# Reordering four pieces of a fused attention and feed-forward block: the turns of y, a maximum's transpose, the pairs' statistics and the adding of y's rows

## The chip, the cores and the metric

The kernel runs on one core of one Trainium2 chip. The metric is the device time in microseconds of the whole program; lower is better. Three runs of the kernel before gave 776.5, 776.8 and 777.04 us, so the median is 776.8 us.

## The reference

The block takes x with 8 batch entries of 1024 rows and 256 columns, all in float32. Cut to what matters:

```python
h = layernorm(x) * (1 + ca) + sa
lhs, rhs = h * w_lhs, h * w_rhs
attn = softmax(einsum('nsd,ntd->nst', lhs, rhs), axis=2)
x = x + ga * einsum('nst,ntd->nsd', attn, h)
h = layernorm(x) * (1 + cb) + sb
y = relu(h @ W1 + b1) @ W2 + b2          # W1: 256 x 1024, W2: 1024 x 256
x = x + gb * y
```

The six rows sa, ca, ga, sb, cb, gb of each batch entry come from a small product of silu(c) and wmod; ga and gb are kept at least 0.25 away from zero.

## The kernel before, in words

**Tiling and order of the work.** A batch entry b (0 to 7) is worked in eight steps i (0 to 7), one for each block of 128 rows. Attention is done for entry b in its own steps; the feed-forward part of entry b-1 is woven into the same steps, its first half of 512 rows in steps 0 to 3 and its second half in steps 4 to 7. So entry b's steps hold attention of b, the feed-forward part of b-1, and the preparation of b+1. Entry 0 has a branch of its own, and the feed-forward part of entry 7 is a tail behind the loop. The order is written out by hand: a program-wide pin at the end ties every instruction to the one before it on its engine, so each engine executes in the order in which the source emits.

**A step in attention.** `direct` (L405, L412) makes the scores of a block that is two steps ahead, from the diagonal to the right. `mirror` (L428) turns that row block on the vector engine into a tile called Tm, and `move` (L295) writes it to DRAM (tile D_m) and reads it back into the column below the diagonal. `row_max` (L455) takes the maximum m of a row, `max_turn` (L460) turns it on TensorE into the PSUM tile pm, `subtract` (L467) and `exponent` (L476) make pT, and `product` (L488) and `product_out` (L502, L504, and the statistics L237, L238) make the new rows of x. In steps 2, 3, 6 and 7 two row blocks are worked together by a seven-product scheme: `pair_begin`, `left_sums`, `pair_end` (the products into pq and pr, L579), `pair_out` (eight vector instructions, L594 to L607) and `pair_stats` (the statistics of the pair, two times L237 and L238).

**A step in the feed-forward part.** In steps 0, 1, 4 and 5 (called "first" in the source) two pairs c of hidden blocks are made: `pair_products` (L713, tiles pa, pb, pc; `kept` is ScalarE's copy of pa), `pair_sums` (four vector instructions, L747, L750, L753, L756), `pair_last` (one product, L764 on the vector engine and L765 on GpSimd), `pair_relu` (L774, L775 on ScalarE) and `pair_turn` (four GpSimd additions, L784 to L787). `pair_products` takes a function `between`, which is the transpose of a maximum when it is given, and calls it right after pa's products. Steps 2, 3, 6 and 7 make y, transposed, in the tile Y (L803 to L838), and `y_turn` (L848) turns it on the vector engine into a tile T_y and moves it through DRAM (D_y) back into Y; `y_add` (L861) adds the rows on GpSimd and `y_out` (L864) stores x.

**Queues and buffers around the change.** All the writes and reads of `move` are issued by SyncE's queue (SP), in program order; a read waits on that queue until its writes have landed. A move with hurry=True issues its read at once, one with hurry=False puts it off until the next move has issued its own read. The tiles that the vector engine turns into (Tm, T_y, T_a, T_f) share one tag with two buffers:

```python
T = two.tile([P, NV, NT * V], F32, tag="T", name=f"T_y{b}_{g}")
```

and the PSUM tiles pa, pb, pc, po, pp, pq, pr and ya to yd share four buffers of the tag "a". In step 3 the tag T is used by Tm and then by T_y; in step 4 by Tm and then by T_a, the turn of the next entry's normalized rows (`prepare_blocks`, L317), which exists only where there is a next entry. In step 4 the vector engine's emitted order is: the sums of pair 0, Tm, L764, T_a, `subtract`, the sums of pair 1, L764, the statistics of the pair made in step 3, the maximum m, `product_out`. Step 5 follows with the second maximum and the sums of pair 2.

Of the kernel before, what the change touches and what calls it, by code (L numbers as in the profile page):

```python
# [24 lines left out]
def adaln_block_kernel(  # L25
# [14 lines left out]
    B, S, D = x.shape  # L40
    INTER = W1.shape[1]
    NT = S // P
# [3 lines left out]
    TH = HALF // P  # L46
    H2 = HALF // 2
    NH = NI // 2
    V = 32
# [245 lines left out]
    def move(out, blocks, m, name, hurry=True):  # L295


        D_ = dram.tile([NV, V, NV, NT * V], F32, tag="D", name=f"D_{name}", bufs=3)
        D_ = D_[:, :, :, 0:m]
        for a in range(NV):  # L300
            nc.sync.dma_start(
                out=D_[:, :, a, :].rearrange("b u m -> u b m"), in_=blocks[ts(a, V)]
            )
        read = lambda: nc.sync.dma_start(out=out, in_=D_.rearrange("b u a m -> (b u) a m"))
        if hurry:
            read()
            read_back()
        else:
            reads.append(read)
# [206 lines left out]
    def right_sums(b, which):  # L516

        xg = xg_t[b]
        b11, b12 = xg[:, 0:TH, P:D], xg[:, 0:TH, 0:P]
        b21, b22 = xg[:, TH:NT, P:D], xg[:, TH:NT, 0:P]  # L520
        t = [tsum[:, n, :, 0:P] for n in range(4)]
        ins = [(b12, b11), (b22, t[0]), (b22, b12), (t[1], b21)]
        for n in which:
            nc.gpsimd.tensor_tensor(t[n], *ins[n], ALU.subtract)

    halves = lambda pT: (pT[:, 0:TH, :], pT[:, TH:NT, :])
    two_t = {}
# [181 lines left out]
    lo, hi = slice(0, H2), slice(H2, HALF)  # L709
    pairs = {}  # L710

    def mm(out, lhsT, rhs):
        nc.tensor.matmul(out, lhsT=lhsT, rhs=rhs, start=True, stop=True)  # L713

    def pair_products(b, g, c, between=None):

        if c == 0:
            ffn["f"] = two.tile([P, NI, HALF], F32, tag="f", name=f"f_{b}_{g}", bufs=1)
            if b < B - 1:
                ffn["ft"] = two.tile([P, 3, NH, H2], F32, tag="ft", name=f"ft_{b}_{g}", bufs=1)  # L720
        hT, hs = ffn["hT", g]
        n = ts(c, P)
        s1, a22 = (w1[:, k, ds((c + NH) * P, P)] for k in range(2))

        pool, tag = (ps_s, "s") if b == B - 1 else (ps_a, "a")
        pa = ps_a.tile([P, HALF], F32, tag="a", name=f"pa_{b}_{g}_{c}")
        pb = pool.tile([P, HALF], F32, tag=tag, name=f"pb_{b}_{g}_{c}")
        pc = ps_a.tile([P, HALF], F32, tag="a", name=f"pc_{b}_{g}_{c}")
        mm(pa[:, lo], w1[:, 0, n], hT[:, 0, lo])
        mm(pa[:, hi], s1, hs[:, 0])  # L730
        kept = work.tile([P, HALF], F32, tag="kept", name=f"kept_{b}_{g}_{c}", bufs=3)
        nc.scalar.copy(kept, pa)  # L732
        if between:
            between()
        mm(pb[:, lo], w1s[:, 0, n], hs[:, 1])
        mm(pb[:, hi], w1s[:, 1, n], hs[:, 2])
        mm(pc[:, lo], w1[:, 1, n], hT[:, 1, lo])
        mm(pc[:, hi], a22, hT[:, 0, hi])
        pairs[c] = pa, pb, pc, kept
# [100 lines left out]
                scale=gcol[:, 0, h, b : b + 1], bias=gcol[:, 1, h, b : b + 1],  # L840
            )

    def y_turn(b, g):

        Y = ffn["Y"]
        T = two.tile([P, NV, NT * V], F32, tag="T", name=f"T_y{b}_{g}")
        for h in range(2):
            nc.vector.transpose(  # L848
                T.rearrange("p a (t h u) -> p a t h u", h=2, u=V)[:, :, :, h, :],
                Y[:, h].rearrange("p (t a v) -> p a t v", a=NV, v=V),  # L850
            )
        Y = Y.rearrange("p h r -> p (h r)").rearrange("p (b m) -> p b m", b=NV)
        move(Y, T, NT * V, f"y{b}_{g}", hurry=False)
        ffn["rows", b, g] = Y.rearrange("p b (t h u) -> p t h b u", h=2, u=V)

    def y_add(b, g, q):
# [278 lines left out]
    for b in range(B):  # L1135
        for i in range(NT):
# [4 lines left out]
            fb, fg = b - 1, i // TH  # L1141
# [54 lines left out]
            if first:  # L1196

                ub, ug = (b - 1, 0) if i >= TH else (b - 2, 1)
                back = i % TH == 0 and ub >= 0
                pair_products(fb, fg, c, turn_max)  # L1200
                if i == 0:
                    ffn_rstd(b - 1, 1)
                elif (b, i) == (B - 1, TH):
                    ffn_rstd(b, 0)
                if (b, i) == (1, 0):
                    weights(*late)
                    late = None
                if c > 0:
                    pair_relu(c - 1)
                pair_sums(fb, fg, c)  # L1210
                if ahead:
                    mirror(*ahead)
                pair_last(fb, fg, c)
                if i == 0:
                    right_sums(b, (3,))
                if c > 0:
                    pair_turn(c - 1)
                if i == 4 and b + 1 < B:
                    prepare_blocks(b + 1, 1)
                    xg_times(b + 1, 1)  # L1220
                if late:
                    subtract(*late)
                pair_products(fb, fg, c + 1, (lambda: max_turn(*extra)) if extra else None)
                pair_relu(c)
                sides_too = i == 4 and b + 1 < B
                if sides_too:
                    prepare_turn_apart(b + 1, 0, 1)
                if late:
                    exponent(*late)
                if sides_too:  # L1230
                    prepare_turn_apart(b + 1, 0, 0)
                middle(b, i)
                pair_sums(fb, fg, c + 1)
                pair_last(fb, fg, c + 1)
                if c == 0 and (b, i - 2) in two_t:
                    pair_stats(b, i - 2)
                if ahead and ahead != extra:
                    row_max(*ahead)
                pair_turn(c)
                if back:  # L1240
                    for q in range(2):
                        y_add(ub, ug, q)
                if i == 5:

                    turns(b, i)
                if c > 0:
                    pair_relu(c + 1)
                    pair_turn(c + 1)
            else:
                half = i % TH - 2  # L1250
                if i == 3 and b + 1 < B:
                    prepare_stats(b + 1, 1)
                if half == 0:
                    pair_begin(b, i, turn_max)
                elif not ahead:

                    pair_end(b, i - 1)
                    pair_out(b, i - 1)
                    pair_stats(b, i - 1)
                if half:  # L1260
                    y_second(fb, fg, turn_max)
                else:
                    y_first(fb, fg)
                if ahead:
                    mirror(*ahead)
                if i == 2 and b + 1 < B:
                    prepare_rstd(b + 1, 0)
                elif i == 3 and b + 1 < B:
                    prepare_rstd(b + 1, 1)
                elif i == 6 and b + 1 < B:  # L1270
                    ffn_rstd(b, 0)
                elif i == NT - 1 and b == B - 1:
                    ffn_rstd(b, 1)
                if half == 0:
                    pair_begin_sum(b, i)
                    if i == 2:
                        weights(*late)
                    left_sums(b, i)
                spare()
                early(b, i)  # L1280
                if late and i != 2:
                    weights(*late)
                middle(b, i)
                if i == 2 and b + 1 < B:
                    load_x(b + 1, 1)
                if i == 3 and b + 1 < B:
                    prepare_norm(b + 1, 1)
                    x_plus(b + 1, 1)
                spare()
                if ahead:  # L1290
                    row_max(*ahead)
                if half:
                    y_second_sums(fb)
                else:
                    y_first_sums()
                spare()
# [5 lines left out]
            if extra:  # L1302
                exponent(*extra)
            if not first:
                if half and b < B - 1 or i == 3:
                    y_turn(fb, fg)
                for _ in range(4 if half else 1):
                    spare()
            if first:
                product(b, i)  # L1310
                product_out(b, i)
            elif half and ahead:
                pair_end(b, i - 1)
                pair_out(b, i - 1)
                if i == NT - 1:
                    assert not queue
                    right_sums(b + 1, range(3))
                if i == NT - 1 or b == B - 1:
                    pair_stats(b, i - 1)
# [84 lines left out]
```

## Time and profile before

| what | value |
|---|---|
| median of three runs | 776.8 us (776.5 to 777.04) |
| profiled execution, its own time | 778.43 us |
| its span, first to last instruction | 776.6 us |
| clock granted to TensorE | 1.00 |
| TensorE products busy | 762.5 us |
| vector engine busy | 575.8 us |
| GpSimd busy | 534.0 us |
| ScalarE busy | 366.4 us |
| DMA | 95.18 MB, mean 123 GB/s |

The profiled execution is one run, 778.43 us in its own timing, of which 776.6 us lie between its first and its last instruction. The page lists busy time and, for groups of instructions, the idle time of the engine just before them and who ended it. The timeline view lists instructions of one engine in order of time, with start and length in us, and in square brackets an idle time before an instruction with its releaser. In this kernel one float32 product of 256 columns shows as two TensorE instructions.

### The profile page before, as it was taken

Reading aid. Unit: us, or ns where it says so; the run is one execution under the profiler, and the core shown is the slowest. Engines: PE = TensorE matmul, PEld = TensorE weight load, DVE = VectorE, ACT = ScalarE, POOL = GpSimd, SP = SyncE. Lnnn points to the kernel's source line nnn. Section 1 sums busy time; section 2 is a strip of 40 time slices with the busy share of each in tenths; the row PEclk is TensorE's granted clock in tenths of the full one; section 3 lists DMA queues with packets and bytes.
Section 4 is the critical chain, followed back from the end, with each engine's and each line's share of the span. In section 5 each row is a group of like instructions: output and inputs, shape, how many; then the busy total and the mean of one; then the engine's idle time right before and its main releaser. Section 6 shows DMA issues by size and latency. Waiting matters only on the chain.

```text
span 776.6 us, 11486 instructions
## 1 busy us (share of the span) xinstructions
PE 762.5 (98%) x3710; PEld 620.6 (80%) x3710; DVE 575.8 (74%) x1238; ACT 366.4 (47%) x671; POOL 534.0 (69%) x626
## 2 busy tenths in 40 slices
PE   8999999999999999999999999999999999999998
PEld 3576788788887888878887888878888788889886
DVE  6597879768796787957888677876879677594632
ACT  4464545535465355544546444553546535251511
POOL 0533895977949688586868778497694968559641
PEclk9999999999999999999999999999999999999999
DMA  5314434355344464434543544435444335232220
GB/s 190 124 28 149 123 103 119 122 167 169 95 128 126 130 177 113 144 104 125 169 126 116 150 149 129 110 121 177 139 121 125 107 122 170 58 103 86 81 82 27
DMA packets 106211, 95.18 MB, mean 123 GB/s; under 512 B 29700, under 2 KB 98848, under 8 KB 106152
## 3 DMA queue, kind: packets, MB, share of 16 engines
q1 hardware_dynamic: 98408, 85.81, 37.8%
q10 hardware_dynamic: 7744, 8.65, 3.5%
q8 instruction: 29, 0.48, 0.2%
q14 instruction: 30, 0.25, 0.1%
HBM read 50.62 MB, written 43.81 MB: 122 GB/s over the span
## 4 chain that ended last, share of the span: by engine, by line
PE 84%; DVE 10%; issue 2%; ACT 2%; POOL 1%; DMA 1%; SPq 0%; DVEq 0%; POOLq 0%
PE psc L405 14%; PE po L488 13%; PE pa L713 8%; PE pb L713 6%; PE yb L791 6%; PE ya L791 6%; PE pc L713 6%; PE yc L791 5%; PE pr L579 4%; PE pp L539 3%; PE py L896 3%; PE pq L579 3%; PE yd L791 3%; DVE pT L467 1%; DVE m L455 1%
## 5 line engine op out<-in xcount | busy, mean ns | idle before, releaser
L765 POOL TENSOR_TENSOR f<-f,kept 128x512 f32<-128x512 f32 x64 | 81.7, 1276 | 118.2 <-DVE f L764 89.6
L405 PE MATMUL psc<-rT,lT 128*128 128x512 f32 (+3 forms) x384 | 134.3, 486 | 0.0
L488 PE MATMUL po<-xg,pT 128*128 128x257 f32 x576 | 131.6, 380 | 0.0
L488 PEld LDWEIGHTS po<-xg,pT 128*128 128x128 f32 x576 | 108.8, 190 | 16.0 <-issue 1.0
L405 PEld LDWEIGHTS psc<-rT,lT 128*128 128x128 f32 x384 | 67.6, 190 | 38.1 <-issue 27.0
L412 ACT COPY sc<-psc 128x512 f32<-128x512 f32 (+3 forms) x96 | 44.8, 474 | 96.5 <-PE psc L405 96.5
L467 DVE TENSOR_TENSOR pT<-sc,pm 128x1024 f32<-128x1024 f32 x64 | 77.1, 1205 | 5.9 <-PE pm L460 5.8
L774 ACT ACTIVATE f<-f 128x512 f32<-128x512 f32 x64 | 40.4, 631 | 83.8 <-POOL f L765 83.8
L476 ACT ACTIVATE pT<-pT 128x1024 f32<-128x1024 f32 x64 | 67.0, 1047 | 26.4 <-DVE pT L467 26.4
L455 DVE TENSOR_REDUCE m<-sc 128x1 f32<-128x1024 f32 x64 | 77.1, 1205 | 0.0
L732 ACT COPY kept<-pa 128x512 f32<-128x512 f32 x64 | 37.4, 585 | 80.7 <-PE pa L713 80.7
L629 POOL TENSOR_TENSOR x<-x,rows 128x256 f32<-128x256 f32 x64 | 45.3, 740 | 37.4 <-ACT rows L1002 23.2
L713 PE MATMUL pb<-hs,w1s 128*128 128x256 f32 x256 | 67.1, 385 | 0.9 <-DVE f L750 0.6
L713 PE MATMUL pc<-hT,w 128*128 128x256 f32 x256 | 66.2, 381 | 0.0
L428 DVE STREAM_TRANSPOSE Tm<-sc 128x896 f32<-128x896 f32 (+6 forms) x49 | 34.7, 707 | 27.6 <-ACT sc L412 27.3
L713 PEld LDWEIGHTS pc<-hT,w 128*128 128x128 f32 x256 | 48.1, 190 | 7.7 <-ACT kept L732 1.4
L713 PEld LDWEIGHTS pb<-hs,w1s 128*128 128x128 f32 x256 | 45.5, 191 | 11.0 <-DVE f L750 4.6
L791 PE MATMUL yc<-f,w2s 128*128 128x256 f32 x224 | 52.1, 379 | 0.0
L791 PEld LDWEIGHTS yc<-f,w2s 128*128 128x128 f32 x224 | 41.5, 190 | 10.1 <-issue 2.9
L786 POOL TENSOR_TENSOR ft<-ft,f 128x256 f32<-128x256 f32 x56 | 41.9, 749 | 4.4
L785 POOL TENSOR_TENSOR ft<-ft,f 128x256 f32<-128x256 f32 x56 | 40.9, 730 | 4.4
L861 POOL TENSOR_TENSOR x<-x,Y 128x512 f32<-128x512 f32 x28 | 35.0, 1272 | 10.6 <-DMA Y<-D_y 10.6
(164 smaller groups left out, 1676.2 us busy)
## 6 DMA issues: line engine op xcount, KB each, us to landing
D_f<-T_f SPq DMA_DIRECT2D x60, 128.0 KB, 2.3
X_f<-D_f SPq DMA_DIRECT2D x15, 512.0 KB, 3.9
D_a<-T_a SPq DMA_DIRECT2D x56, 128.0 KB, 3.5
D_y<-T_y SPq DMA_DIRECT2D x56, 128.0 KB, 2.8
Y<-D_y SPq DMA_DIRECT2D x14, 512.0 KB, 3.9
out_dram<-x SPq DMA_DIRECT2D x14, 512.0 KB, 4.3
X_a<-D_a SPq DMA_DIRECT2D x13, 512.0 KB, 3.4
x<-in_L_attn_x_dram ACTq DMA_DIRECT2D x12, 512.0 KB, 3.8
```

Of the source, the lines that this page charges most:

```text
L405: nc.tensor.matmul(psc[:, : hi - lo], lhsT=lT_t[b, i // TH][:, k, ts(i % TH, P)], rhs=rT_t[b, n][:, k, lo - n * HALF : HALF], start=(k == ...
L412: nc.scalar.copy(score_row(b, i)[:, lo // V : hi // V, :], psc[:, : hi - lo].rearrange("p (n v) -> p n v", v=V),)
L455: nc.vector.tensor_reduce(m, score_row(b, i), AX.XY, ALU.max)
L467: nc.vector.tensor_tensor(pT.rearrange("p j (a v) -> p j a v", v=V), score_columns(b, i), pm[:, :P].rearrange("p (j a v) -> p j a v", j=1, ...
L476: nc.scalar.activation(pT_t[b, i], pT_t[b, i], AF.Exp)
L488: nc.tensor.matmul(po[:, : D + 1], lhsT=pT[:, t, :], rhs=xg_t[b][:, t, 0 : D + 1], start=(t == 0), stop=(t == NT - 1),)
L579: nc.tensor.matmul(out, lhsT=lhs[:, t, :], rhs=rhs[:, t, :], start=(t == 0), stop=(t == TH - 1),)
L629: queue.append(lambda: nc.gpsimd.tensor_tensor(out, in0, row, op))
L713: nc.tensor.matmul(out, lhsT=lhsT, rhs=rhs, start=True, stop=True)
L765: nc.gpsimd.tensor_tensor(f[:, c::NH, hi], f[:, c::NH, hi], kept[:, None, hi].to_broadcast([P, 2, H2]), ALU.add,)
L786: add(ft[:, 2, c], ft[:, 1, c], f[:, c + NH, lo], ALU.subtract)
L791: nc.tensor.matmul(out, lhsT=lhs(c), rhs=rhs(c), start=(c == 0), stop=(c == NH - 1))
```

## The change

The change touches only the order of emission. `pair_products` calls `between` after pb's two products and not before them. The statistics of the pair of step 3 (`pair_stats(b, 2)`) are emitted behind `product_out` of step 4 and no longer ahead of the maximum of step 4. In step 3 `y_turn` is emitted behind `pair_end` and `pair_out`, with its read put off as before; in step 7 it stays where it was, but its read is issued at once. In step 0 `y_add` moves from the end of the step to just behind `pair_last` of pair 0, `right_sums(b, (3,))` moves behind `pair_turn` of pair 0, and the relu and turn of pair 1 move from step 1 into step 0.

```diff
@@ pair_products
         nc.scalar.copy(kept, pa)
+        mm(pb[:, lo], w1s[:, 0, n], hs[:, 1])
+        mm(pb[:, hi], w1s[:, 1, n], hs[:, 2])
         if between:
             between()
-        mm(pb[:, lo], w1s[:, 0, n], hs[:, 1])
-        mm(pb[:, hi], w1s[:, 1, n], hs[:, 2])
@@ y_turn
-    def y_turn(b, g):
+    def y_turn(b, g, hurry=False):
...
-        move(Y, T, NT * V, f"y{b}_{g}", hurry=False)
+        move(Y, T, NT * V, f"y{b}_{g}", hurry)
@@ steps 0, 1, 4, 5
-                if c > 0:
+                if i == TH + 1:
                     pair_relu(c - 1)
                 pair_sums(fb, fg, c)
                 if ahead:
                     mirror(*ahead)
                 pair_last(fb, fg, c)
-                if i == 0:
-                    right_sums(b, (3,))
-                if c > 0:
+                if i == 0 and back:
+                    for q in range(2):
+                        y_add(ub, ug, q)
+                if i == TH + 1:
                     pair_turn(c - 1)
...
                 pair_last(fb, fg, c + 1)
-                if c == 0 and (b, i - 2) in two_t:
-                    pair_stats(b, i - 2)
                 if ahead and ahead != extra:
                     row_max(*ahead)
                 pair_turn(c)
-                if back:
+                if i == 0:
+                    right_sums(b, (3,))
+                    pair_relu(c + 1)
+                    pair_turn(c + 1)
+                elif back:
                     for q in range(2):
                         y_add(ub, ug, q)
@@ ends of the steps
             if not first:
-                if half and b < B - 1 or i == 3:
-                    y_turn(fb, fg)
+                if i == NT - 1 and b < B - 1:
+                    y_turn(fb, fg, True)
...
             if first:
                 product(b, i)
                 product_out(b, i)
+                if (b, i - 2) in two_t:
+                    pair_stats(b, i - 2)
             elif half and ahead:
                 pair_end(b, i - 1)
                 pair_out(b, i - 1)
+                if i < NT - 1:
+                    y_turn(fb, fg)
```

## The prediction

> **What bounds the kernel now.** I read the page's busy times first, then the list of waits for TensorE, then the timelines of TensorE, the vector engine and SyncE around steps 3 to 5.
>
> ```profile
> PE 762.5 (98%) x3710; PEld 620.6 (80%) x3710; DVE 575.8 (74%) x1238; ACT 366.4 (47%) x671; POOL 534.0 (69%) x626
> ```
>
> TensorE sets the time: what does not open or close one of its pauses moves nothing. From the list of waits (total us, times, longest):
>
> ```profile
> PE pm L460 <- DVE m L455: 3.9, 6, 1.1
> PEld pm L460 <- DVE m L455: 6.9, 7, 1.5
> PEld pb L713 <- DVE f L750: 4.6, 13, 0.8
> ```
>
> The pauses of entries 1 to 7 recur in two places. At entry 6, TensorE's timeline shows:
>
> ```profile
> 591.58 1.13 PE L713 MATMUL pb<-hs,w1s 128*128 128x256 f32 x4
> ...
> 598.18 0.59 PE L713 MATMUL pa<-hs,w 128*128 128x256 f32 x2
> 599.29 0.32 PE L460 MATMUL pm<-ident,m 128*128 128x128 f32 x1 [0.51 <-DVE m L455]
> ...
> 602.47 0.27 PE L460 MATMUL pm<-ident,m 128*128 128x128 f32 x1
> 602.59 1.13 PE L713 MATMUL pb<-hs,w1s 128*128 128x256 f32 x4
> ```
>
> A two-instruction group takes 0.43 us where nothing waits, so pm was due at 598.61: **0.67 us lost** at step 5. The pb at 591.58 (pair 1) came 0.21 us late, and the first half of a pb that waited costs 0.1 us more (1.13 against 1.03). The pb at 602.59 (pair 3) bears that mark too. The vector engine in the same stretch:
>
> ```profile
> 586.51 1.42 DVE L848 STREAM_TRANSPOSE T_y<-Y 128x512 f32<-128x512 f32 x2 [1.05 <-ACT Y L838]
> 587.85 0.26 DVE L594 TENSOR_TENSOR W<-pq,W 128x129 f32<-128x129 f32 x1
> ...
> 590.46 0.48 DVE L747 SCALAR_TENSOR_TENSOR u<-pb,cols,kept 128x256 f32<-128x256 f32 x1
> ...
> 592.70 1.29 DVE L317 STREAM_TRANSPOSE T_a<-xg 128x512 f32<-128x512 f32 x2
> ...
> 598.05 1.19 DVE L455 TENSOR_REDUCE m<-sc 128x1 f32<-128x1024 f32 x1
> ...
> 602.05 0.48 DVE L750 SCALAR_TENSOR_TENSOR f<-pb,b_step,u 128x256 f32<-128x256 f32 x1
> ```
>
> From T_y to L750 of pair 2, which ends at 602.53, the engine works without a pause. pb of pair 3 starts 0.06 us after that end. So it is **the vector engine's queue**, not the one maximum, that holds TensorE in steps 4 and 5. Entry 7 shows the same wait openly:
>
> ```profile
> 694.91 1.13 PE L713 MATMUL pb<-hs,w1s 128*128 128x256 f32 x4 [0.59 <-DVE f L750]
> ```
>
> A small natural experiment stands in entry 5, where T_a waited for its buffer:
>
> ```profile
> 500.32 1.30 DVE L317 STREAM_TRANSPOSE T_a<-xg 128x512 f32<-128x512 f32 x2 [0.51 <-DMA D_y<-T_y]
> ```
>
> There T_a came 7.78 us after the step's last product group (pr<-xg, 492.54) against 7.19 at entry 6 (585.51), 0.59 more; and TensorE's pause at pm was 1.28 against 0.67 us, 0.61 more. A late T_a is paid for one to one. In the trace, L750 of pair 2 ends 9.84 to 9.86 us after T_a's start in all of entries 1 to 6.
>
> **What the Trainium skill says.** "Perfetto Trace Analysis", section Optimization Strategy, says that a gap which repeats on the engine that should be saturated can mean too few buffers for the next tile. The trace agrees twice: pb waits for a PSUM buffer that L750 frees, T_a for one that D_y frees. "DMA: Bandwidth & Descriptors", section Anatomy of one DMA, puts about 2.0 us of fixed cost on a DMA, most of it the receipt of the last byte; it measured GpSimd's path. Here, from SyncE, the four 128 KB writes of D_y in step 3 show a median of 2.3 us to landing. "Trainium Architecture — The Big Picture", section Inside one NeuronCore, gives each engine its own instruction stream; the trace agrees in that everything behind the waiting T_a moved with it.
>
> **The change, part by part.**
>
> *The maximum's transpose two products later.* pm is due 4 × 0.216 = 0.86 us later (588.25 to 589.12 is one such pb group), enough for the 0.67 us. But pb of pair 3 then asks for its buffer earlier, and that buffer comes from L750 of pair 2, behind everything on the vector engine. Worth nothing by itself. pm of step 5's second maximum now also stands behind that pb, so its 0.11 us no longer lies in the pause: +0.11 us for each of entries 1 to 7.
>
> *Statistics later.* Two pairs of L237 and L238, 1.08 us (596.97 to 598.05), leave the place ahead of m of step 4, and land ahead of the second m (600.42). Both places lie before L750 of pair 2: zero at pb.
>
> *y's turn behind the pair's sums, step 3.* This decides.
> 1. `pair_out` can start as soon as TensorE is done. In step 7 the sums already stand so: pr<-xg at 632.32, L595 at 633.41 (1.09 us later), end 635.73 (2.32 us on). For entry 6: 585.51 + 1.09 + 2.32 = 588.92.
> 2. T_y follows: 1.34 us (1.42 less 0.08 of overlap), end 590.26. u of pair 0 is then due at 590.19 against 590.46, so L750 of pair 0 ends 0.27 us sooner and the pause of 0.21 + 0.10 at pair 1's pb goes.
> 3. SyncE issues D_y when T_y is done; before, that was at 587.96:
>
> ```profile
> 587.96 1.78 SPq L301 DMA_DIRECT2D D_y<-T_y  x4
> ```
>
> Now it is 590.29. The last of four starts about 1.3 us in and lands 2.26 us later (2.3 in the view), and T_a starts 0.1 us after that: 3.67 us, 593.95.
> 4. T_a would be due at 592.43, and waits 1.5 us. It starts 1.25 us later than before. Behind it on the vector engine stand `subtract`, the sums of pair 1, m, `product_out`, the statistics, the second m and the sums of pair 2; TensorE waits for m (at pm) and for L750 (at pb of pair 3). L750 of pair 2 ends at 593.95 + 9.84 = 603.79, pb of pair 3 starts near 603.85 instead of 602.59. What pair 1's pb saved is waited away there.
>
> The same sum, 8.44 us after pr<-xg, against the trace's own T_a in entries 1 to 6 (7.18, 7.31, 7.18, 7.41, 7.78, 7.19): +1.26, +1.13, +1.26, +1.03, +0.66, +1.25, in all **+6.6 us**. With 6 × 0.11 it is +7.3.
>
> *Entry 7* has no T_a, but its T_y lay in a hole, as these two lines show:
>
> ```profile
> 675.40 1.42 DVE L848 STREAM_TRANSPOSE T_y<-Y 128x512 f32<-128x512 f32 x2 [0.47 <-DMA sc<-D_m]
> 678.07 0.29 DVE L594 TENSOR_TENSOR W<-pq,W 128x129 f32<-128x129 f32 x1 [1.26 <-PE pq L579]
> ```
>
> Behind the sums its 1.34 us push the statistics and u of pair 0. Pair 1's pb started at 683.63, 0.16 us after L750's end, so it loses about 1.3, and the pauses of step 5 stay: **+1.4 us** with pm's 0.11.
>
> *y's rows at once, y_add in step 0.* D_y of step 7 has landed by about 636.9 at entry 7; read at once, with the page's 3.9 us, Y is there at 640.9. GpSimd ends L765 of pair 0 at 642.17, so y_add finds it ready. It takes 2.5 us and puts L765 of pair 1 from 644.31 to about 644.7; the relu moved behind it ends near 647.4, before the next score copy is needed at 647.78. SyncE's read leaves its place ahead of D_f and waits in step 7, where its queue issued nothing from 633.77 to the next mirror at 640.48. TensorE has no pause in steps 0 to 3 that could be won, entries 2 to 7. Zero; if Y landed 1 us later, ScalarE would delay copies by that, and the vector engine has 0.8 us of slack there (u at 649.69). I keep 0 to +0.5 us an entry as the far end. `right_sums(3)` is needed three steps later: zero.
>
> **Sum:** 7.3 + 1.4 = +8.7 us. On the profiled execution's 778.43 us (span 776.6) that is 787.1; it stood 1.6 us over the median, so on the median **785.5 us**.
>
> Bounds. A D_y write took at least 2.1 us in the trace, 0.16 less: −1 us. In step 7 the median was 3.3 us, with a mirror's read of 384 KB in flight; in the new place of step 3 the 128 KB read before it is over and a small D_m follows, so I allow half that excess: +3 us. Entry 7 may hide its share: −1.4. Anything that makes T_a wait less than I say, another 2 us.
>
> **The rivals.**
> - *T_a is not held* (its buffer free in time). Then only the shorter hole counts: L750 moves −0.26 to −0.86 by entry, −2.5 in all; with pm +0.8 and entry 7's 1.34 it ends at 776.4. Against it: entry 5's wait. Chance 0.04.
> - *Faster: pb of pair 3 does not hang on L750 of pair 2*, and pm alone held TensorE. Place: that pb; for it speaks that at entry 6 no idle time stands before it. Then m moves by 1.25 − 1.08 = +0.17, pm by 0.86 less 0.32: a rest of some 0.3 us, so each entry gains 0.65 (0.9 and 1.3 at entries 4 and 5), 4.8 us, less 1.4: 773.4. It decides if that pb may start more than 1.3 us before L750 ends. Entry 7's line speaks against it. Chance 0.08.
> - *Slower still*: D_y lands as late as in step 7 everywhere, +6 us: 791.5. Part of the slower case.
>
> **How the numbers follow.** Some 0.2% (1.6 us) is what a measurement can tell. Held T_a, slower: 0.88. Faster 0.08. Within 0.2%: 0.04. The range takes the bounds above: 781.0 to 789.0.
>
> **What would show it.** Right: in entries 1 to 6 T_a waits about 1.5 us for D_y<-T_y; pb of pair 3 waits about 2 us for L750 in step 5; pb of pair 1 in step 4 waits no more, except at entry 7; y_add follows L765 with no wait in step 0. Wrong: T_a without a wait, or no pause at pair 3's pb, or new pauses in steps 0 to 2.

## The result, and the profile after

The changed kernel takes 794.56 us in the median of six runs (791.01 to 795.83), against 776.65 us for six runs of the kernel before: 17.9 us more by the medians; the ratio of the means is 1.022 (95% interval 1.0205 to 1.0236). The forecast was 785.5 us with a range of 781 to 789. The direction was right, and the size was half of what came. The profiled execution took 795.12 us; its span is 793.3 us, 16.7 us over the span before, and its mean granted clock is 0.989, where it was 1.000.

The vector engine's timeline at entry 6, the counterpart of the one shown before (start, length, what; in brackets idle time and its releaser):

```profile
598.34 0.29 DVE L594 TENSOR_TENSOR W<-pq,W 128x129 f32<-128x129 f32 x1 [0.29 <-PE pq L579]
599.23 0.42 DVE L595 TENSOR_TENSOR W<-pr,W 128x256 f32<-128x256 f32 x1 [0.60 <-PE pr L579]
...
601.47 1.30 DVE L848 STREAM_TRANSPOSE T_y<-Y 128x512 f32<-128x512 f32 x2
602.70 0.44 DVE L747 SCALAR_TENSOR_TENSOR u<-pb,cols,kept 128x256 f32<-128x256 f32 x1
...
606.53 1.30 DVE L317 STREAM_TRANSPOSE T_a<-xg 128x512 f32<-128x512 f32 x2 [1.56 <-DMA D_y<-T_y]
...
610.82 1.21 DVE L455 TENSOR_REDUCE m<-sc 128x1 f32<-128x1024 f32 x1
...
615.91 0.48 DVE L750 SCALAR_TENSOR_TENSOR f<-pb,b_step,u 128x256 f32<-128x256 f32 x1
```

The turn stands behind the sums, and T_a waits 1.56 us for the writes of D_y. SyncE issues them as T_y ends:

```profile
602.80 1.74 SPq L301 DMA_DIRECT2D D_y<-T_y  x4
```

From there to T_a are 3.73 us; the forecast took 3.67. TensorE's timeline shows the two pauses of step 5, a short one at pm and a long one at pb, and something else behind the second:

```profile
610.88 1.03 PE L713 MATMUL pb<-hs,w1s 128*128 128x256 f32 x4
612.09 0.32 PE L460 MATMUL pm<-ident,m 128*128 128x128 f32 x1 [0.19 <-DVE m L455]
...
616.45 1.59 PE L713 MATMUL pb<-hs,w1s 128*128 128x256 f32 x4 [1.88 <-DVE f L750]
617.83 0.42 PE L460 MATMUL pm<-ident,m 128*128 128x128 f32 x1
618.04 1.92 PE L713 MATMUL pc<-hT,w 128*128 128x256 f32 x4
```

pb of pair 3 waits for L750, as forecast. It starts 2.25 us after the product ahead of it, which needs 0.216 us where nothing waits, so 2.03 us are lost. (The view's 1.88 us of idle time is less, because its modelled end of a product lies later than the next one could have started. Below, a pause is what is lost, unless idle time is named.) But a group of four that takes 1.03 us elsewhere takes 1.92 here. The view by windows, which has TensorE's granted clock in the column after POOL's count, gives the reason:

```profile
core 0: us, PE busy (x) PEld busy (x) DVE busy (x) ACT busy (x) POOL busy (x), PEclk, DMA share, GB/s
613.57:616.97 3.40, 1.52 (x7) 1.03 (x6) 3.30 (x9) 0.58 (x1) 3.32 (x5) 1.00 0.37 115
616.98:620.38 3.40, 3.40 (x10) 2.66 (x9) 2.86 (x6) 1.36 (x3) 3.32 (x4) 0.50 0.80 287
620.40:623.80 3.40, 3.40 (x17) 2.98 (x17) 3.19 (x6) 2.31 (x4) 3.32 (x5) 1.00 0.00 0
...
139.11:142.52 3.41, 1.73 (x9) 1.50 (x10) 3.38 (x7) 0.48 (x1) 3.41 (x4) 1.00 0.46 154
142.53:145.93 3.40, 3.40 (x17) 3.01 (x16) 3.37 (x8) 2.57 (x4) 3.24 (x5) 1.00 0.46 154
```

For 3.41 us after the pause TensorE ran at half clock, and ran 10 instructions where the next stretch of that length has 17. The trace has five such stretches, in entries 2 to 6, each behind the pause of step 5. Entry 1, whose lines are the last two, has the same pause of 2.03 us and no such stretch. **The page does not show this**: its row of 40 slices, each of some 20 us, prints 9 for the clock in every slice, before and after.

### The profile page after: what moved, and what is told of

The parts are those of the page before. It is cut to its first block, busy times and chain, and to the rows that moved or that the text cites. A ratio compares the mean times of both kernels' runs of the same rounds, so it can differ in the third digit from the quotient of the medians.

```text
span 793.3 us, 11480 instructions
## 1 busy us (share of the span) xinstructions
PE 769.8 (97%) x3710; PEld 627.4 (79%) x3710; DVE 573.7 (72%) x1238; ACT 369.1 (47%) x671; POOL 532.5 (67%) x626
## 4 chain that ended last, share of the span: by engine, by line
PE 78%; DVE 12%; issue 3%; POOL 2%; DMA 2%; ACT 1%; SPq 1%; DVEq 0%; POOLq 0%
PE psc L405 14%; PE po L488 12%; PE yc L791 6%; PE pa L713 6%; PE ya L791 6%; PE yb L791 6%; PE pb L713 5%; PE pc L713 5%; PE pr L579 5%; PE pq L579 3%; PE py L896 3%; PE yd L791 3%; PE pp L539 3%; DMA D_y<-T_y 2%; DVE m L455 1%
## 5 line engine op out<-in xcount | busy, mean ns | idle before, releaser
L713 PE MATMUL pb<-hs,w1s 128*128 128x256 f32 x256 | 69.6, 396 | 13.2 <-DVE f L750 13.1
L713 PE MATMUL pc<-hT,w 128*128 128x256 f32 x256 | 70.2, 399 | 0.0
L713 PEld LDWEIGHTS pb<-hs,w1s 128*128 128x128 f32 x256 | 48.6, 194 | 23.6 <-DVE f L750 16.8
L701 POOL TENSOR_TENSOR hs<-hT 128x256 f32<-128x256 f32 x16 | 11.7, 728 | 54.6 <-DVE hT L692 54.6
```

## The experiments

**e1_three_buffers** takes the suspected wait away with the change left in place: with three buffers in turn T_a no longer takes the one of T_y. The third buffer is written in all three places where the tag T is used, of which one is shown; `kept` gives one of its buffers up to make room.

```diff
-    T = two.tile([P, NV, NT * V], F32, tag="T", name=f"T_y{b}_{g}")
+    T = two.tile([P, NV, NT * V], F32, tag="T", name=f"T_y{b}_{g}", bufs=3)
...
-    kept = work.tile([P, HALF], F32, tag="kept", name=f"kept_{b}_{g}_{c}", bufs=3)
+    kept = work.tile([P, HALF], F32, tag="kept", name=f"kept_{b}_{g}_{c}", bufs=2)
```

> The changed kernel with three buffers for the tag T instead of two, so that T_a does not take T_y's buffer; to make room, kept has two buffers instead of three. Theory: the loss is T_a's wait for D_y plus TensorE's half clock after the pause that this makes. Then T_a stands about 6.9 us behind the last product group of step 3 instead of 8.4, the pause at pair 3's pb shrinks from 2.0 to under 0.6 us, no stretch of half clock is left, and the time is 775 to 778 us. Rival (the loss comes from the other three moves: pm later, statistics later, step 0): T_a does not wait, but the time stays above 785 us.

777.28 us, a ratio to before of 1.0012 (1.0005 to 1.0018). T_a stands 6.76 us behind the last product group of step 3 in every entry, without a wait, and the trace has no stretch of half clock behind a pause. At entry 6 (the vector engine, then TensorE):

```profile
587.46 1.30 DVE L848 STREAM_TRANSPOSE T_y<-Y 128x512 f32<-128x512 f32 x2
...
590.88 1.29 DVE L317 STREAM_TRANSPOSE T_a<-xg 128x512 f32<-128x512 f32 x2
```

```profile
600.77 1.13 PE L713 MATMUL pb<-hs,w1s 128*128 128x256 f32 x4 [0.66 <-DVE f L750]
```

All but some 0.7 us of the 17.9 us (777.28 less 776.63 in this comparison) go with this one buffer; the smaller `kept` was not run alone. The pause at pair 3's pb is 0.83 to 0.85 us (1.18 in entry 3) rather than under 0.6. It stays because the vector engine's queue from T_a to the end of L750 of pair 2 is as long as before: 9.84 us in five entries, 10.19 in entry 3.

**e2_turn_alone** is the kernel before with the turn of step 3 moved, and nothing else.

```diff
-                if half and b < B - 1 or i == 3:
+                if i == NT - 1 and b < B - 1:
                     y_turn(fb, fg)
...
                 pair_out(b, i - 1)
+                if i < NT - 1:
+                    y_turn(fb, fg)
```

> The kernel before with one part of the change alone: y's turn of step 3 behind the pair's sums. Theory: T_a waits as in the changed kernel, 8.4 us behind the last product group of step 3; the pause shows at pm of step 5 as one of about 2.2 us, as the statistics still stand ahead of that maximum, and the half clock follows in most entries: 790 to 795 us. Rival (the other moves make the loss): 777 to 780 us.

793.39 us, ratio 1.0218 (1.0191 to 1.0244), which is the changed kernel's within the interval: the loss comes with this move alone. T_a stands 8.27 to 8.39 us behind. With the statistics still ahead of m, and pm still ahead of pb, the wait shows at pm (2.19 to 2.27 us), and half clock follows in entries 2, 3, 4 and 6. At entry 6:

```profile
609.64 0.32 PE L460 MATMUL pm<-ident,m 128*128 128x128 f32 x1 [2.10 <-DVE m L455]
609.80 1.84 PE L713 MATMUL pb<-hs,w1s 128*128 128x256 f32 x4
611.43 1.91 PE L713 MATMUL pc<-hT,w 128*128 128x256 f32 x4
```

**e3_turn_back** is the changed kernel with that one move undone.

```diff
-                if i == NT - 1 and b < B - 1:
-                    y_turn(fb, fg, True)
+                if half and b < B - 1 or i == 3:
+                    y_turn(fb, fg, i == NT - 1)
...
-                if i < NT - 1:
-                    y_turn(fb, fg)
```

> The changed kernel with y's turn of step 3 back ahead of the pair's sums; the other three parts stay. Theory: L750 of pair 2 comes as in the kernel before, pb of pair 3 waits about 0.7 us in the place of pm, no half clock: 777 to 778 us, so the other three parts are worth 0 to +1 us. Rival (the other parts cost): 780 to 788 us.

778.33 us, ratio 1.0020 (1.0011 to 1.0028), a third of a microsecond over the expected span. The other three parts together cost 1.7 us (0.9 to 2.2 by the interval) and win nothing. The trace is of a run of 776.46 us, the second shortest of twenty (776.03 to 780.35), so it does not tell where the 1.7 us go. In it, pm no longer waits, and pb of pair 3 waits in its place:

```profile
597.39 0.27 PE L460 MATMUL pm<-ident,m 128*128 128x128 f32 x1
...
600.51 1.13 PE L713 MATMUL pb<-hs,w1s 128*128 128x256 f32 x4 [0.68 <-DVE f L750]
```

**e4_fill** leaves the wait for the vector engine as it is and gives TensorE work inside the pause. What its expectation calls the monitor of TensorE's clock is described in the section on why the prediction was wrong.

```diff
+        for n_ in range(fill):
+            pw = ps_s.tile([P, HALF], F32, tag="s", name=f"pw_f{b}_{g}_{c}_{n_}")
+            mm(pw, ident, w1[:, n_ % 2, 0:HALF])
         mm(pb[:, lo], w1s[:, 0, n], hs[:, 1])
...
+                    2 if i == 5 and b < B - 1 else 0,
```

The last line is the new argument of the second `pair_products` of a step: two products in step 5 of entries 1 to 6, ahead of pair 3's pb.

> The changed kernel, which in step 5 of entries 1 to 6 issues two more 512-column products that nobody reads, ahead of pair 3's pb: 1.7 us of work inside the pause of 2.0 us. The wait on the vector engine is the same. Theory (the monitor of TensorE's clock sees the pause): no stretch of half clock, 785 to 787 us. Rival (the slow products come from data arriving late or from traffic): the products after the pause stay slow, 794 us or more.

788.63 us, ratio 1.0153 (1.0134 to 1.0172). The clock is 1.000, there is no stretch of half clock, and the products behind the pause are quick again (L753 is here what L750 is elsewhere, as the edit adds three lines):

```profile
610.64 1.88 PE L713 MATMUL pw_f<-w,ident 128*128 128x512 f32 x4
612.68 1.13 PE L713 MATMUL pb<-hs,w1s 128*128 128x256 f32 x4 [0.16 <-DVE f L753]
613.65 0.27 PE L460 MATMUL pm<-ident,m 128*128 128x128 f32 x1
613.75 1.03 PE L713 MATMUL pc<-hT,w 128*128 128x256 f32 x4
```

So with more products to do the kernel is 5.9 us faster than the changed one. The wait for the vector engine is still there, and the slow products went with the pause. Traffic does not tell them apart: the DMA share in the 3.4 us from 611.90 is 0.44 at full clock, and in the five slow stretches of the changed kernel it is 0.40 to 0.80. The time is 1.6 us over the expected span, and why is open. The profiled run, 790.68 us, is the longest of the four; the waits of T_a in its entries 3 and 6 (2.76 and 2.34 us) were longer than in the changed kernel's trace (1.58 and 1.56), though T_y stood at the same place, so D_y landed later there. That is about what sets this run apart from the other three (787.7 to 788.76).

**e7_pm_alone** is the kernel before with only the transpose moved behind pb's two products.

> The kernel before with the maximum's transpose two products later alone. Theory: the pause of 0.67 us at pm of step 5 turns into one of the same length at pb of pair 3, plus 0.11 us an entry: 776.6 to 777.8 us. Rival (pm was the bound): 771 to 773 us.

777.44 us, ratio 1.0006 (0.9998 to 1.0014): no difference. In four entries the pause of 0.67 us at pm turned into one of 0.84 us at pair 3's pb; in entry 2 it was 0.66, in entry 6 0.19, where T_a stood earlier (6.57 and 6.13 us behind the last product group).

**e8_step0_alone** is the kernel before with only the parts of steps 7, 0 and 1: y's rows read at once, `y_add` behind pair 0, `right_sums`, relu and turn of pair 1 in step 0.

> The kernel before with the step 0 part alone: y's rows read at once, added behind pair 0, and the relu and turn of pair 1 in step 0. Theory: hidden, 776.2 to 777.2 us. Rival (GpSimd's or ScalarE's queue holds something in step 0 or 1): 778 us or more.

777.32 us, ratio 1.0003 (0.9995 to 1.0012): 0.1 us over the expected span, and no difference that these runs can tell. In the changed kernel's trace, too, `y_add` starts without a wait in step 0 of every entry.

**e5_stats_step5** asks whether the vector engine's queue up to L750 of pair 2 is the bound. It is the kernel before with pm moved, and the statistics taken out of the stretch altogether, to the end of step 5.

```diff
-                if c == 0 and (b, i - 2) in two_t:
-                    pair_stats(b, i - 2)
...
                 product_out(b, i)
+                if (b, i - 3) in two_t:
+                    pair_stats(b, i - 3)
```

> The kernel before with the transpose two products later and the pair's statistics moved to the end of step 5, behind its product_out, so that 1.08 us of vector work leave the stretch ahead of L750 of pair 2. Theory (the vector engine's queue up to L750 of pair 2 bounds steps 4 and 5): L750 comes 1.1 us sooner, neither pm nor pair 3's pb waits in entries 1 to 6, the pause of 0.3 us at pair 1's pb stays: 770.5 to 772.5 us. Rival (the queue is not the bound, the maximum alone is): as e7_pm_alone.

772.47 us, ratio 0.9942 (0.9930 to 0.9954): faster. L750 of pair 2 now ends 8.78 us behind T_a (9.05 in entry 6), where it was 9.84 to 9.86. No pause over 0.05 us is left at pm or at pair 3's pb in entries 1 to 6; the 0.21 us at pair 1's pb stay. At entry 6:

```profile
594.23 0.27 PE L460 MATMUL pm<-ident,m 128*128 128x128 f32 x1
...
596.55 1.13 PE L713 MATMUL pb<-hs,w1s 128*128 128x256 f32 x4
```

e7 has the first half of this edit alone and gained nothing, so the gain is that of the statistics. The change had moved the same four instructions, but to a place that is still ahead of L750.

**e6_best** adds to e5_stats_step5 the third buffer and, in entries 1 to 6 only, the turn behind the sums. The part for the turn is shown.

```diff
-                if half and b < B - 1 or i == 3:
+                if (half and b < B - 1) if i == NT - 1 else (i == 3 and b == B - 1):
                     y_turn(fb, fg)
...
                 pair_out(b, i - 1)
+                if i == 3 and b < B - 1:
+                    y_turn(fb, fg)
```

> The kernel of e5_stats_step5 with three buffers for T (kept has two) and y's turn of step 3 behind the pair's sums in entries 1 to 6 alone. Theory: the turn's 0.27 us come through once T_a is not held, pair 1's pb waits no more, and the waits of T_a in entries 4 and 5 are gone: 768 to 770.5 us. Rival: nothing left to win beyond e5_stats_step5, 771 us or more.

770.42 us, ratio 0.9917 (0.9905 to 0.9929), the fastest of all and 24.1 us below the changed kernel. TensorE runs through step 5 without a mark of a wait:

```profile
591.91 1.03 PE L713 MATMUL pb<-hs,w1s 128*128 128x256 f32 x4
592.77 0.27 PE L460 MATMUL pm<-ident,m 128*128 128x128 f32 x1
...
595.04 1.03 PE L713 MATMUL pb<-hs,w1s 128*128 128x256 f32 x4
```

In its trace each of entries 1 to 6 takes 91.11 us from the last product group of one step 3 to that of the next. Before, it was 92.35 to 92.97.

## Why the prediction was wrong in size, and what of it was right

**Right: the mechanism and its place.** T_a came 8.31 to 8.42 us behind the last product group in five of six entries (8.81 in entry 5), where the sum had 8.44. L750 of pair 2 ends 9.85 or 9.86 us after T_a starts, as before. pb of pair 3 waits 2.03 us in each entry. The natural experiment of entry 5 had told this. pb of pair 1 waits no more in entries 1 to 6. T_a's shifts against the kernel before are 1.13, 1.09, 1.23, 0.97, 1.03 and 1.21 us, together 6.7 against 6.6 forecast.

**Right: that the other parts win nothing.** e7 and e8 bear out two of the zeros in the working within the noise, and pm's pause moved to pb of pair 3, as it said. The third zero, of the statistics, was not run alone. The three together cost 1.7 us in e3, where the working had 0.11 us an entry, 0.8 in all; the rest is open.

**Slightly off: entry 7.** From its last product group of step 3 to the end it takes 99.81 us against 98.76: +1.05, not +1.45. Pair 1's pb lost 0.96 us there and not 1.3:

```profile
699.12 0.47 DVE L747 SCALAR_TENSOR_TENSOR u<-pb,cols,kept 128x256 f32<-128x256 f32 x1
```

u starts 5.60 us behind that group (693.52 in the trace). Before, it was 4.55 (682.42 less 677.87), so the turn pushed it by 1.05 us and not by 1.34: T_y takes 1.30 us here, and overlaps a little with both of its neighbours.

**Wrong: a missing term.** The step that failed is the one from waits to time. The working says that what does not open or close one of TensorE's pauses moves nothing, and its sum prices a pause at its length. It put at nothing, without a reason, what TensorE's clock does after one; that is about half of the loss. The sum over the two traces: from entry 1's to entry 7's last product group of step 3 the kernel before takes 555.13 us and the changed one 570.95, +15.8. Of it 6.7 is T_a's shift and 0.66 is pm. The remaining 8.5 us are five stretches of 3.41 us at half clock, each worth half its length, 5 × 1.71 = 8.5. That closes the gap, and it closes by entry too: counted from one step 3 to the next, entry 1, without a stretch, is 1.26 us longer than before, and entries 2 to 6 are 2.76 to 3.04 us longer. With entry 7's 1.05 us the traces' whole difference of 16.7 us is told (entry 0 is 0.2 us shorter). e4 shows the cause, e1 and e2 where the pause comes from. The upper bound of the range, and the rival of 791.5 us, had no such case either: they let D_y land late, and T_a was no more than 0.4 us later than the sum had it (in entry 5).

The Trainium skill has this term: "TensorE: Matmul & The Clock Gate", section "Part 1: The HAM clock gate", describes a monitor of how busy TensorE is, with a free-running window of about 3.4 us, that halves the clock after an idle window. The trace agrees with the length (3.41 us) and with the free running: the four intervals between the stretches are 95.57 or 95.58 us, 28 times 3.413. Its section "Why this matters for your kernels" puts the danger at pauses over some 3 us. Here 2.03 us were enough, so the measurement decides: from the starts of the stretches the windows can be laid out, and those with a pause of 2.03 to 2.27 us in them (1.87 to 2.11 us idle in the view) were followed by half clock (nine of nine, in the changed kernel and e2), those with 1.68 to 1.81 us (three) were not. Entry 1's pause of 2.03 us was split by a window's border into 1.68 and a rest, and went free. This layout was read from two traces; no run was made to move a pause across a border, so where the limit lies, and that the border decides, is argued and not shown.

The shortest runs of the changed kernel (791.01 us, twice) have a mean clock of 0.996 where the others have 0.989 to 0.991, so probably fewer of their entries were hit; there is no trace of them that could show it. The clock does not account for the whole spread of 4.8 us: the longest run, 795.83 us, has 0.991, and the profiled one, 795.12 us, has 0.989.

## What to carry to other kernels

In a queue that is full from end to end, moving an instruction later helps only if it passes the last thing that someone waits for; the change moved the statistics past one waiter and not past the next, and e5 moved them past both. Before a tile's writer is moved later, look up who takes its buffer next: the release moves with it, and the next user may stand at the head of a busy queue. And a pause of TensorE that grows from under one to two microseconds can cost nearly double its length (here 2.03 us and 1.7 us more), so price the clock behind it as well.

## What the runs showed of the hardware

A pause of 2.03 us in a kernel that keeps TensorE 97% busy drew 3.41 us of half clock, worth 1.7 us, in five entries of six. Pauses of 0.7 to 1.3 us (before, e1, e3) drew none. Two products of 512 columns in each of six pauses, which nobody reads, kept the clock at 1.000 and made the kernel 5.9 us faster. In the changed kernel entries 2 to 6 took 95.36 to 95.80 us from one step 3 to the next, close to 28 windows (95.57 us), so that the pause began at nearly the same place of its window in each of them, 1.0 to 1.4 us behind the border.
